# A two-layer graph network on one core: edge groups taken in descending order throughout, node steps in the same iteration, the last four node blocks step by step together

## The chip, the core and the metric

The kernel runs on one core of a Trainium2 chip. Its engines work side by side: TensorE (PE, with PEld for its weight loads) multiplies matrices into PSUM, VectorE (DVE) and ScalarE (ACT) do elementwise work, GpSimd (POOL) issues the indirect DMAs that gather rows, and SyncE (SP) issues plain DMAs, as ACT does too. The metric is the device time of one launch in microseconds; less is better.

## The reference

There are N = 30000 nodes with D = 128 features and E = 960000 edges, sorted by their destination. Layer 0 is a pair of relational graph convolutions with 32 relations built from 8 bases. Layer 1 is a gated convolution with 4 edge types.

```python
dst = minimum((30000 * uniform(960000) ** 2.0).astype(int32), 29999)   # then sorted
# convolution of layer 0, twice, with relu between:
W = einsum('rb,bdf->rdf', coeff, basis)
msg = einsum('nd,rdf->nrf', h, W)[src, etype] * norm
agg = segment_sum(msg, dst, num_segments=N) + bias
# layer 1, for each of T = 4 types:
k, q, v = x @ Wk[t] + bk[t], x @ Wq[t] + bq[t], x @ Wv[t] + bv[t]
msg = where(edge_type == t, sigmoid(k[dst] + q[src]) * v[src], 0)
out_t = segment_sum(msg, dst) + x @ Ws[t] + b[t]
# the result is the mean over t; both layers take relu(layernorm(x)) and add x
```

## The kernel before

**Tiles and groups.** Edges come in tiles of 128, three tiles (G = 3) make a group of GE = 384 edges, and there are NGR = 2500 groups. Edges are sorted by destination, so a group's destinations lie within a window of W = 32 nodes. Sums live in `agg`, one SBUF tile of 128 features by NX columns, a column per node; `add_windows` (L356) adds the 32-column result of a group to the columns that start at the group's first destination. Those starts are read from memory into registers (`bases`, L345), so DVE knows them only at run time.

**Passes.** `edge_pass` (L296) runs three times: c1 (first convolution), c2 (second) and g (gated layer). Each is a hardware loop (L312) of NI = 25 iterations with NG = 100 groups each. In an iteration of c1 and c2 (`rel_body`), each group gathers its three tiles of rows with one indirect DMA a tile (`gather`, L113; 15,000 in the two passes), builds selection matrices on DVE (L439), multiplies on PE (L445), copies on ACT (L449), and for every five groups multiplies with the bases (L407) and adds five windows (L359). In g (`gate_body`), each group gathers rows of `qvtab` (7,500 in all), forms keys (L499), adds, takes the sigmoid (L541), multiplies (L508), sums by destination (L510) and adds windows.

**Node steps.** When the sums of a node are complete, its columns have to be turned into rows and prepared for the next pass. That is done in blocks of VB = 120 nodes, and each pass has its own list of steps with a position for each: `after_first` (L556) adds a bias, takes relu, transposes, stores rows of `h1` and resets the columns to x plus a bias; `after_second` (L587) takes the layer norm and computes the tables `ktab` and `qvtab` with three 512-wide multiplications; `after_third` (L673) transposes and stores the output. An iteration carries NPI / VB = 10 blocks: block u's steps stand beside groups u x PERIOD + n, with PERIOD = 9 and n the step's position (L317 to L325). The order inside an iteration is written out by hand (`manual_schedule`); tile pools give the number of buffers.

**Order.** The host reverses the 25 stretches of edges, so that iteration 0 has the edges with the highest destinations; inside a stretch the groups ascend. An iteration's node blocks cover nodes whose sums were completed by earlier iterations: block u of iteration i starts at column N + LAG + 120 u - 1200 i, with LAG = 240. In iteration 0 those columns lie above N, in padding. After the loop the lowest NPI + LAG = 1440 columns are left: 12 blocks, taken one after another in program order (L328 to L332), with three buffers for most tiles (two for `xt` and `xs`) and six PSUM banks. POOL has no gathers to issue in that time, and the next pass reads the tables that the last blocks write.

**A check ahead.** Before the passes, the kernel tests on the chip that the destinations allow this order (L227 to L249): all of a group's destinations within its window, and no stretch's last group reaching columns that were already worked off. If a test fails, a general path (`any_path`, L732) runs instead of `sorted_path`.

Of the kernel before, what the change touches and what calls it, by code (L numbers as in the profile page):

```python
# [44 lines left out]
VB = 120  # L45
NPI = N // NI
PERIOD = NG * VB // NPI - 1
LAG = 2 * VB
NX = N + NPI + LAG
GAP = 8  # L50
EPS = 1e-5
CH = 5
# [17 lines left out]
def kernel(  # L70
# [114 lines left out]
    with tc.tile_pool(name="prep", bufs=2) as prep, tc.tile_pool(name="pre", bufs=4) as pre, \  # L185
            tc.tile_pool(name="prep_ps", bufs=1, space=PSUM) as prep_ps:
        lo = prep.tile([TP, CH], F32, name="lo", bufs=1)
        hi = prep.tile([TP, CH], F32, name="hi", bufs=1)

        def edge_chunk(c):  # L190
            ts = slice(c * CT, (c + 1) * CT)
            fi = prep.tile([TP, CG], I32, name="fi")
            nc.sync.dma_start(fi, rows_of(first[c * CG:(c + 1) * CG], TP))
            dch = prep.tile([TP, CT], I32, name="dch")
            nc.sync.dma_start(dch, dst[:, ts])
            rch = prep.tile([TP, CT], F32, name="rch")
            nc.vector.tensor_tensor(
                rch.rearrange("p (g j) -> p g j", j=G),
                dch.rearrange("p (g j) -> p g j", j=G),
                fi.unsqueeze(2).to_broadcast([TP, CG, G]),  # L200
                ALU.subtract,
            )
            nc.vector.tensor_reduce(lo[:, c:c + 1], rch, AX.X, ALU.min)
            nc.vector.tensor_reduce(hi[:, c:c + 1], rch, AX.X, ALU.max)
            nc.scalar.dma_start(reld[:, ts], rch)

        def node_chunk(i):
            xt = pre.tile([P, KN, D], F32, name="xt")
            nc.sync.dma_start(xt, step(x, i))
            st = pre.tile([P, KN, 6], F32, name="st")  # L210
            mv = pre.tile([P, KN, 2], F32, name="mv")
            for k in range(KN):
                nc.vector.bn_stats(st[:, k, :], xt[:, k, :])
                nc.vector.bn_aggr(mv[:, k, :], st[:, k, :])
            rs = pre.tile([P, KN], F32, name="rs")
            nc.scalar.activation(rs, mv[:, :, 1], AF.Sqrt, bias=eps)
            nc.vector.reciprocal(rs, rs)
            off = pre.tile([P, KN], F32, name="off")
            nc.vector.scalar_tensor_tensor(off, mv[:, :, 0], -1.0, rs, op0=ALU.mult,
                                           op1=ALU.mult)  # L220
            h = pre.tile([P, KN, D], F32, name="h")
            for k in range(KN):
                nc.scalar.activation(h[:, k, :], xt[:, k, :], AF.Relu, scale=rs[:, k:k + 1],
                                     bias=off[:, k:k + 1])
            nc.scalar.dma_start(step(h0, i), h)

        for c in range(CH):  # L227
            edge_chunk(c)
            for i in range(c * STEPS // CH, (c + 1) * STEPS // CH):
                node_chunk(i)  # L230
        bad = prep.tile([TP, 2, CH], F32, name="bad", bufs=1)
        nc.vector.tensor_scalar(bad[:, 0, :], lo, 0.0, None, op0=ALU.is_lt)
        nc.vector.tensor_scalar(bad[:, 1, :], hi, float(W - 1), None, op0=ALU.is_gt)
        nbad = prep.tile([TP, 1], F32, name="nbad", bufs=1)
        nc.vector.tensor_reduce(nbad, bad, AX.XY, ALU.add)
        at = prep.tile([NI, NG], I32, name="at", bufs=1)
        nc.sync.dma_start(at, first.rearrange("(i g) -> i g", i=NI))
        last = prep.tile([NI, 1], F32, name="last", bufs=1)
        nc.vector.tensor_reduce(last, at, AX.X, ALU.max)
        even = prep.tile([NI, 1], F32, name="even", bufs=1)  # L240
        nc.gpsimd.iota(even, pattern=[[0, 1]], base=N + LAG - W, channel_multiplier=-NPI,
                       allow_small_or_imprecise_dtypes=True)
        late = prep.tile([NI, 1], F32, name="late", bufs=1)
        nc.vector.tensor_tensor(late, last, even, ALU.is_gt)
        nc.vector.tensor_add(nbad[:NI], nbad[:NI], late)
        pbad = prep_ps.tile([1, 1], F32, name="pbad")
        nc.tensor.matmul(pbad, lhsT=nbad, rhs=ones[:TP], start=True, stop=True)
        nc.vector.tensor_copy(flag, pbad)
    n_bad = nc.values_load(flag[0:1, 0:1], min_val=0, max_val=2 * CH * TP + NI)  # L249


    def node_weights(nodew):
# [39 lines left out]


    def sorted_path():
        with ExitStack() as all_:
            def edge_pass(name, body, after, banks, extra=None):  # L296


                with ExitStack() as held:
                    weights = held.enter_context(tc.tile_pool(name=f"{name}_w", bufs=1))  # L300
                    steps, run = after(weights), body(weights)
                    with tc.tile_pool(name=f"{name}_io", bufs=NQ) as io, \
                            tc.tile_pool(name=f"{name}", bufs=2) as pool, \
                            tc.tile_pool(name=f"{name}_n", bufs=1) as npool, \
                            tc.tile_pool(name=f"{name}_nps", bufs=banks, space=PSUM) as nps, \
                            tc.tile_pool(name=f"{name}_c", bufs=1, space=PSUM) as cps, \
                            tc.tile_pool(name=f"{name}_ps", bufs=2, space=PSUM) as ps:
                        cp = cps.tile([P, 4 * D], F32, name="cp")
                        iw, ic = cp[:, :W], cp[:, W:W + 1]
                        nc.vector.tensor_copy(iw, irow)  # L310
                        nc.vector.tensor_copy(ic, icol)
                        with tc.For_i(0, NI, 1, iteration_sync="staggered") as i:  # L312
                            with tc.manual_schedule():
                                todo = {}
                                for n, step_ in extra(i, npool) if extra else ():
                                    todo.setdefault(n, []).append(step_)
                                for u in range(NPI // VB):  # L317
                                    at = i * -NPI + (N + LAG + u * VB)
                                    for n, step in steps(at, npool, nps):
                                        todo.setdefault(u * PERIOD + n, []).append(step)  # L320
                                assert W < TQ * 4 * B and max(todo) < NG

                                def beside(n):
                                    for step in todo.get(n, ()):
                                        step()  # L325

                                run(i, io, pool, ps, cp, iw, ic, beside)
                    with tc.tile_pool(name=f"{name}_l", bufs=3) as lpool, \  # L328
                            tc.tile_pool(name=f"{name}_lps", bufs=6, space=PSUM) as lps:
                        for at in range(0, NPI + LAG, VB):  # L330
                            for _, step in steps(at, lpool, lps):
                                step()  # L332

            def leave_stage():
# [220 lines left out]

            def after_first(weights):  # L556

                def steps(at, pool, ps):
                    xt = pool.tile([VB, D], F32, name="xt", bufs=2)
                    r = pool.tile([P, VB], F32, name="r")  # L560
                    h = pool.tile([VB, D], F32, name="h")
                    cols, rows = agg[:, ds(at, VB)], ds(at, VB)
# [24 lines left out]
            def after_second(weights):  # L587
# [6 lines left out]
                nc.vector.tensor_reduce(bsc, b4, AX.X, ALU.add)  # L594
                nc.vector.tensor_scalar(bsc, bsc, 1.0 / T, None, op0=ALU.mult)

                def steps(at, pool, ps):
                    cols, rows = agg[:, ds(at, VB)], ds(at, VB)
                    xs = pool.tile([P, VB], F32, name="xs", bufs=2)
                    st = pool.tile([VB, 6], F32, name="st")  # L600
                    mv = pool.tile([VB, 2], F32, name="mv")
                    rs = pool.tile([VB, 1], F32, name="rs")
# [69 lines left out]

            def after_third(weights):  # L673

                def steps(at, pool, ps):
                    c = pool.tile([P, VB], F32, name="c")
                    o = pool.tile([VB, D], F32, name="o")
                    got = {}

                    def copy():  # L680
                        nc.scalar.copy(c, agg[:, ds(at, VB)])  # L681

                    def turn():
                        got["pr"] = ps.tile([VB, D], F32, name="pr")
                        nc.tensor.transpose(got["pr"], c, ident)  # L685

                    def back():
                        nc.scalar.copy(o, got["pr"])  # L688

                    def store():  # L690
                        nc.scalar.dma_start(out[ds(at, VB), :], o)  # L691

                    return (1, copy), (3, turn), (4, back), (5, store)
# [268 lines left out]
```

## Time and profile before

| | us |
|---|---|
| median of three timed runs | 28902.54 (28895.52 to 28908.87) |
| the profiled execution's own time | 34449.25 |
| its span | 34447.5 |
| stretch of c1's loop (215 to 11386) | 11171 |
| stretch of c2's loop (11432 to 22748) | 11316 |
| stretch of g's loop (22865 to 34420) | 11555 |
| mean granted PE clock | 0.674 |

The span runs from the first to the last instruction of one recorded execution. That execution is longer than the timed ones; its durations and the order of its events are what the views show. In lines of the views, L445 is line 445 of the kernel, `out<-in` are tile names, "xN" is a count, and square brackets give the idle time of the engine ahead of an instruction with what ended it. "issue" is idle time in which nothing shown was waited for, and "remote" is a releaser that the record does not name.

### The profile page before, as it was taken

What the parts mean: (1) busy time and instruction counts of PE and PEld (TensorE: products, weight loads), DVE (VectorE), ACT (ScalarE), POOL (GpSimd) and SP (SyncE); (2) the same over time, 40 slices, a digit from 0 to 9 for tenths busy, and PEclk for the clock granted to TensorE, in tenths of its full rate; (3) what the DMA queues carried; (4) which work ended last, traced back from release to release, by engine and by line L of the source; (5) the groups of instructions that cost most, each with busy time, mean ns of one, the idle gap of its engine ahead of it and who ended that gap; (6) DMA issues with size and microseconds to landing.
All of it is one profiled execution on the core that took longest, in us unless ns stands there. A gap on an engine that the chain in (4) does not pass through costs nothing. (4 is left out here: it accounts for less than half of the span.)

```text
span 34447.5 us, 320361 instructions
## 1 busy us (share of the span) xinstructions
PE 20497.2 (60%) x87408; PEld 17662.1 (51%) x87408; DVE 12592.8 (37%) x33274; ACT 3659.3 (11%) x9905; POOL 21410.1 (62%) x22514
## 2 busy tenths in 40 slices
PE   4555555555555566666666666665555555555555
PEld 3444544444444445545555454445555555555555
DVE  3333333333333333333333333333333333333333
ACT  1000000000000111111111111111111111111111
POOL 5666666666666566666666666656666666666666
PEclk7777777777777777777777777765555555555555
DMA  3222222222222222222222222234444444444444
GB/s 97 62 62 62 63 61 62 63 63 62 62 62 62 70 73 73 73 74 72 72 73 73 73 73 73 73 107 145 145 144 144 144 144 146 145 144 144 146 143 141
DMA packets 2182999, 3244.35 MB, mean 94 GB/s; under 512 B 551918, under 2 KB 1559594, under 8 KB 2181290
## 3 DMA queue, kind: packets, MB, share of 16 engines
q0 software_dynamic: 840000, 1967.52, 20.6%
q1 hardware_dynamic: 993620, 1001.65, 9.0%
q10 hardware_dynamic: 347670, 254.20, 2.6%
q8 instruction: 852, 13.96, 0.2%
q14 instruction: 857, 7.02, 0.1%
HBM read 2969.29 MB, written 252.28 MB: 94 GB/s over the span
## 5 line engine op out<-in xcount | busy, mean ns | idle before, releaser
L114 POOL DMA_INDIRECT hg<-h,idx x15000 | 14273.0, 952 | 8446.5 <-issue 4105.1
L445 PE MATMUL pa<-sb,hg 128*128 128x256 f32 x30000 | 9304.2, 468 | 5934.2 <-issue 2892.9
L445 PEld LDWEIGHTS pa<-sb,hg 128*128 128x128 f32 x30000 | 6919.2, 240 | 7715.2 <-issue 3346.1
L114 POOL DMA_INDIRECT qv<-qvtab,qi x7500 | 7109.3, 948 | 4562.6 <-issue 2220.3
L439 DVE SCALAR_TENSOR_TENSOR sb<-cp,relc,ce 128x256 f32<-128x256 f32 x15000 | 6134.1, 476 | 6576.0 <-remote 4679.9
L510 PE MATMUL po<-sel,msg 128*128 128x32 f32 x15000 | 3471.0, 388 | 4592.1 <-DVE msg L508 3824.5
L510 PEld LDWEIGHTS po<-sel,msg 128*128 128x128 f32 x15000 | 3420.4, 328 | 4894.5 <-DVE msg L508 3986.6
L499 PE MATMUL pk<-kw,kb 128*128 128x128 f32 x15000 | 3973.5, 438 | 219.5 <-DVE kb L486 178.4
L540 DVE TENSOR_TENSOR pk<-pk,qv 128x384 f32<-128x384 f32 x2500 | 1406.8, 563 | 7074.9 <-remote 4837.9
L449 ACT COPY ab<-pa 128x256 f32<-128x256 f32 x5000 | 1816.6, 373 | 20148.8 <-remote 8809.6
L499 PEld LDWEIGHTS pk<-kw,kb 128*128 128x128 f32 x15000 | 3466.7, 331 | 222.3 <-issue 222.3
L407 PE MATMUL po<-ab,bas 128*128 128x160 f32 x16000 | 2431.3, 306 | 311.2 <-ACT ab L449 262.8
L407 PEld LDWEIGHTS po<-ab,bas 128*128 128x128 f32 x16000 | 2356.8, 196 | 408.4 <-ACT ab L449 291.0
L359 DVE TENSOR_TENSOR agg<-agg,po 128x32 f32 x7500 | 1402.9, 187 | 2742.5 <-remote 709.7
L541 ACT ACTIVATE pk<-pk 128x384 f32<-128x384 f32 x2500 | 1186.7, 475 | 9493.7 <-DVE pk L540 6531.3
L390 PE MATMUL cp<-coeff,oh 128*128 128x32 f32 x8000 | 1313.4, 297 | 1472.0 <-issue 1173.2
L390 PEld LDWEIGHTS cp<-coeff,oh 128*128 128x128 f32 x8000 | 1394.2, 237 | 1530.9 <-issue 1308.1
L637 PE MATMUL bank<-wall,hT 128*120 128x512 f32 x1572 | 1012.0, 765 | 710.2 <-issue 307.3
L508 DVE TENSOR_TENSOR msg<-pk,qv 128x384 f32<-128x384 f32 x2500 | 1368.0, 548 | 19.4 <-remote 19.4
L486 DVE TENSOR_TENSOR kb<-kb,cp 128x1920 f32<-128x1920 f32 x500 | 1072.7, 2145 | 52.0 <-issue 29.6
L637 PEld LDWEIGHTS bank<-wall,hT 128*120 128x120 f32 x1572 | 345.9, 235 | 988.0 <-issue 581.2
L648 DVE TENSOR_TENSOR kt<-bank,ball 120x512 f32<-120x512 f32 x262 | 181.2, 692 | 1484.0 <-remote 509.2
(77 smaller groups left out, 3762.9 us busy)
## 6 DMA issues: line engine op xcount, KB each, us to landing
kb<-kcode SPq DMA_DIRECT2D x500, 960.0 KB
er<-in_et_row SPq DMA_DIRECT2D x1000, 256.0 KB
hg<-h,idx POOLq DMA_INDIRECT x15000
kw<-ktab SPq DMA_DIRECT2D x2500, 64.0 KB
qvtab<-qvt ACTq DMA_DIRECT2D x262, 480.0 KB
qv<-qvtab,qi POOLq DMA_INDIRECT x7500
ktab<-kt ACTq DMA_DIRECT2D x262, 240.0 KB
xt<-in_x SPq DMA_DIRECT2D x262, 60.0 KB
```

Of the source, the lines that this page charges most:

```text
L114: nc.gpsimd.indirect_dma_start(out=to, out_offset=None, in_=table, in_offset=bass.IndirectOffsetOnAxis(ap=idx, axis=0))
L359: nc.vector.tensor_add(to, to, po[:, g, :])
L390: nc.tensor.matmul(pc[s][:, c].rearrange("p q b -> p (q b)"), lhsT=oh[s][:, c, :], rhs=cof.rearrange("p q b -> p (q b)"), start=True, stop ...
L407: nc.tensor.matmul(po[s].rearrange("p s w -> p (s w)"), lhsT=bas[:, b, :], rhs=ab[s][:, b].rearrange("p s w -> p (s w)"), start=(b == 0), ...
L439: nc.vector.scalar_tensor_tensor(sb, iw[:TP].unsqueeze(1).to_broadcast([TP, B, W]), relc[:, t0 + j:t0 + j + 1], ce[s].rearrange("p q c b - ...
L445: nc.tensor.matmul(pa.rearrange("p b w -> p (b w)"), lhsT=hg[:, j, :], rhs=sb.rearrange("p b w -> p (b w)"), start=(j == 0), stop=(j == G ...
L449: nc.scalar.copy(ab[s][:, :, g, :], pa)
L499: nc.tensor.matmul(pk[n][:, j, :], lhsT=kb[n // S][:, n % S, j * TP:(j + 1) * TP], rhs=kw[n], start=True, stop=True)
L508: nc.vector.tensor_mul(msg, pk[n], qv[n][:, :, 1, :])
L510: nc.tensor.matmul(po[s][:, g, :], lhsT=msg[:, j, :], rhs=sel[s][:, g * G + j, :], start=(j == 0), stop=(j == G - 1))
L540: nc.vector.tensor_add(pk[n], pk[n], qv[n][:, :, 0, :])
L637: nc.tensor.matmul(bank(a, VB, T * D), lhsT=hT, rhs=wall[:, a].rearrange("p t f -> p (t f)"), start=True, stop=True)
```

## The change

The host reverses the order of all 2500 groups, not that of 25 stretches, so destinations descend from group to group within an iteration as well. The node blocks follow inside the same iteration: block u of iteration i starts at column N + LAG - 120 (u + 1) - 1200 i, with LAG = 480. An assertion on the host says that the blocks stay behind the additions by at most LEAD = 360 columns. The test on the chip compares every group's first destination with its own limit, where it compared each stretch's highest one. After the loop 480 columns are left, 4 blocks, and they are taken together: the first step of all four, then the second step of all four, and so on, with four buffers for each tile and eight PSUM banks.

```diff
-LAG = 2 * VB
-NX = N + NPI + LAG
+LAG = 4 * VB
+NX = N + LAG
+LEAD = 3 * VB
...
-        last = prep.tile([NI, 1], F32, name="last", bufs=1)
-        nc.vector.tensor_reduce(last, at, AX.X, ALU.max)
-        even = prep.tile([NI, 1], F32, name="even", bufs=1)
-        nc.gpsimd.iota(even, pattern=[[0, 1]], base=N + LAG - W, channel_multiplier=-NPI,
-                       allow_small_or_imprecise_dtypes=True)
+        even = prep.tile([NI, NG], F32, name="even", bufs=1)
+        nc.gpsimd.iota(even, pattern=[[-NPI // NG, NG]], base=N + LAG - LEAD - W,
+                       channel_multiplier=-NPI, allow_small_or_imprecise_dtypes=True)
+        nc.vector.tensor_tensor(even, at, even, ALU.is_gt)
         late = prep.tile([NI, 1], F32, name="late", bufs=1)
-        nc.vector.tensor_tensor(late, last, even, ALU.is_gt)
+        nc.vector.tensor_reduce(late, even, AX.X, ALU.add)
...
+        for u in range(NPI // VB):
+            late = min(g for g in range(NG)
+                       if min((g // S + 2) * S + S - 2, NG) > u * PERIOD + 1)
+            assert (u + 1) * VB - late * NPI // NG <= LEAD
...
                                 for u in range(NPI // VB):
-                                    at = i * -NPI + (N + LAG + u * VB)
-                                    for n, step in steps(at, npool, nps):
+                                    at = i * -NPI + (N + LAG - (u + 1) * VB)
+                                    for n, step in steps(at, npool, nps, 2):
                                         todo.setdefault(u * PERIOD + n, []).append(step)
...
-                    with tc.tile_pool(name=f"{name}_l", bufs=3) as lpool, \
-                            tc.tile_pool(name=f"{name}_lps", bufs=6, space=PSUM) as lps:
-                        for at in range(0, NPI + LAG, VB):
-                            for _, step in steps(at, lpool, lps):
+                    left = LAG // VB
+                    with tc.tile_pool(name=f"{name}_l", bufs=left) as lpool, \
+                            tc.tile_pool(name=f"{name}_lps", bufs=8, space=PSUM) as lps:
+                        for together in zip(*(steps(at, lpool, lps, left)
+                                              for at in range(0, LAG, VB))):
+                            for _, step in together:
                                 step()
...
-                def steps(at, pool, ps):
-                    xt = pool.tile([VB, D], F32, name="xt", bufs=2)
+                def steps(at, pool, ps, deep):
+                    xt = pool.tile([VB, D], F32, name="xt", bufs=deep)
...
-                def steps(at, pool, ps):
+                def steps(at, pool, ps, deep):
...
-                    xs = pool.tile([P, VB], F32, name="xs", bufs=2)
+                    xs = pool.tile([P, VB], F32, name="xs", bufs=deep)
...
-        return np.ascontiguousarray(v.reshape(NI, -1)[::-1]).reshape(-1)
+        return np.ascontiguousarray(v.reshape(NGR, GE)[::-1]).reshape(-1)
```

More of the change, by code (lines that the diff above doesn't have):

```diff
@@ L248 @@
         nc.vector.tensor_copy(flag, pbad)
-    n_bad = nc.values_load(flag[0:1, 0:1], min_val=0, max_val=2 * CH * TP + NI)
+    n_bad = nc.values_load(flag[0:1, 0:1], min_val=0, max_val=2 * CH * TP + NGR)
     def node_weights(nodew):
@@ L673, in after_third, with steps @@
             def after_third(weights):
-                def steps(at, pool, ps):
+                def steps(at, pool, ps, deep):
                     c = pool.tile([P, VB], F32, name="c")
```

## The prediction

> **What bounds the kernel now.** First the head of the page: which engine sets the pace, and is it the same one throughout?
>
> ```profile
> PE 20497.2 (60%) x87408; PEld 17662.1 (51%) x87408; DVE 12592.8 (37%) x33274; ACT 3659.3 (11%) x9905; POOL 21410.1 (62%) x22514
> ...
> POOL 5666666666666566666666666656666666666666
> PEclk7777777777777777777777777765555555555555
> ```
>
> No engine is full, and POOL holds one level through all three passes: it issues 22,500 gathers. The wait table of POOL says what lies between them.
>
> ```profile
> POOL hg L114 <- issue: 4105.1, 12309, 164.1
> POOL qv L114 <- issue: 2220.3, 6716, 4.5
> POOL hg L114 <- remote: 1988.1, 816, 3.8
> POOL qv L114 <- DVE msg L508: 1761.6, 473, 15.1
> ...
> POOL qv L114 <- DMA qi<-qidx: 121.1, 3, 117.2
> ...
> POOL hg L114 <- DMA idx<-in_src: 44.5, 1, 44.5
> ```
>
> The columns are total us, times, longest. Two lines hold one very long wait each: 44.5 and 117.2 us. The timeline of POOL puts them at 11387.4 to 11431.9 and at 22748.0 to 22865.2, between one pass and the next. They are the places where the blocks left over after a loop are worked off, with no gather to run beside them. The view by stretches, cut there (columns: us; busy time and instructions of PE, PEld, DVE, ACT, POOL; PE clock; DMA share; GB/s):
>
> ```profile
> 11395.00:11412.00 17.00, 7.68 (x24) 3.64 (x24) 4.06 (x12) 6.78 (x24) 0.00 (x0) 0.53 0.32 84
> 11412.00:11432.00 20.00, 0.00 (x0) 0.00 (x0) 3.26 (x10) 0.00 (x0) 0.13 (x1) 0.50 0.50 129
> 22748.00:22756.00 8.00, 3.78 (x20) 2.80 (x20) 1.88 (x10) 1.25 (x5) 0.03 (x1) 0.98 0.03 10
> 22756.00:22856.00 100.00, 64.85 (x120) 27.49 (x120) 31.59 (x86) 15.79 (x47) 0.00 (x0) 0.73 0.33 84
> 22856.00:22865.00 9.00, 0.00 (x0) 0.00 (x0) 0.00 (x0) 0.00 (x0) 0.00 (x0) 0.61 0.26 66
> 34430.00:34448.00 18.00, 4.48 (x12) 2.11 (x12) 0.00 (x0) 6.87 (x25) 0.00 (x0) 0.50 0.20 47
> ```
>
> So the left-over blocks cost about 17 us after c1, 100 us after c2 and 18 us after g, all with POOL at zero. In c2 the blocks go one after another; one of the twelve in the timeline:
>
> ```profile
> 22783.76 5.47 PE L637 MATMUL bank<-wall,hT 128*120 128x512 f32 x6 [0.36 <-ACT hT L633]
> ...
> 22789.27 0.69 DVE L648 TENSOR_TENSOR qvt<-bank,ball 120x512 f32<-120x512 f32 x1 [2.72 <-PE bank L637]
> ...
> 22790.12 0.29 DVE L620 BATCH_NORM_STATS2 st<-bank 120x6 f32<-120x128 f32 x1
> ...
> 22791.52 0.41 DVE L626 TENSOR_SCALAR hn<-bank,mv,rs 120x128 f32<-120x128 f32 x1
> ...
> 22792.34 0.27 ACT L633 ACTIVATE hT<-bank 128x120 f32<-128x120 f32 x1 [0.88 <-PE bank L630]
> ...
> 22792.67 0.75 PE L637 MATMUL bank<-wall,hT 128*120 128x512 f32 x1 [0.36 <-ACT hT L633]
> ```
>
> The next block's statistics (22790.12) start only after this block's weights, and its own weights at 22792.67, 8.9 us after this one's. PE waits through norm, turn and relu every time.
>
> [...] six weight matmuls of a left-over block take 5.47 us in some blocks and 2.84 us in others, a ratio of 1.93. [...] Here 84 GB/s filled a share of 0.33, thus an estimated 255 GB/s when full. [...] loops are fetched anew: the instruction queues q8 and q14 moved 20.98 MB[...]. [...] ACT_TABLE_LOAD: [...] the trace has 1283, once ahead of g's left-over blocks, and it stays.
>
> **Part by part.** The sum is against the profiled execution (34449.25 us, span 34447.5). The runs' median is 28902.54, 5546.7 us less, or 0.247 us for each of the 22,500 gathers. I take this as recording cost of the gathers; the left-over blocks have none, so their savings count in full in both.
>
> *Loops.* Per iteration there are ten blocks before and after, at the same places (u x PERIOD + n, PERIOD still 9), with the same instructions; only the constant in the row address differs, and bufs=2 is what they had. The DMAs of a moved block (xt on SP, stores on ACT) are the same, on the same queues, past the same instructions. Two things might change. First, blocks now read columns that this iteration's adds have just written. But the trace of before already makes them wait: "ACT c L681 <- DVE agg L359" 40 times, 38.6 us together, though those columns lay outside this iteration's windows. Ordering goes by the tile, so no new wait: 0. Cover if wrong: a block's copy stands at n = 1 + 9u, adds at n = 3, 8, 13... (4, 9, 14... in g), mostly a group or more earlier; a group is 3 gathers, 3.75 us. Second, the order of groups: same counts, sizes, and still random sources: 0. Placement of the later loops' code: bound below.
>
> *Preparation.* The agg memset shrinks by 960 of 31440 columns (26.3 us x 3% = 0.8), on POOL, idle until 192 us. The test on "at" has three instructions either way (0.235 + 0.147 + 0.122 us before); a 25x100 compare is of the size of the 0.235. Sum: 0.
>
> *After c1.* Before: 11395.06 (first xt load) to 11411.65 (end of the last store), 16.6 us, paced by xt loads with two buffers. After: four loads at once. The first landed after 3.6 us, the second 0.47 later; four at this step land by 5.1. Then transpose 0.46, DVE 0.34, last store issue 0.34, with hand-overs 0.2: about 6.5. Saves 10 (8 to 11).
>
> *After c2.* Before: 22755.67 to 22856.02, 100.35 us. After, by phases of four blocks, in us from the first copy:
> - copies and transposes; DVE's first statistics at 2.7 as before (an unexplained idle that I keep);
> - statistics 4 x (0.33 + 0.21) = 2.2, to 4.9; norm 4 x (0.20 + 0.41) = 2.4, to 7.3; last turn and relu to 7.8;
> - 24 weight matmuls. The twelve blocks took 2.84 to 5.47 for six, mean 4.58. [...] I take 3.75 a block: 15.0. The bounds are 4 x 2.84 = 11.4 and 4 x 5.47 = 21.9. Four "part" at 0.4: 1.6. PE ends at 24.4;
> - biases and copies (4 x 2 x 0.69 on DVE, 4 x 0.59 on ACT) lie beside PE; store issues, 8 x 0.90 = 7.2 on ACT, half beside it, and the last qvtab issue ends at about 27.5.
>
> Eight banks carry it: the first reuse is w0 on px's bank, released at norm. Drain: four blocks are 2.88 MB; the last 1.92 MB at 255 GB/s take 7.5 us, of which 3 stick out. 100.35 - 27.5 - 3 = 70 (62 to 78). Late next is the loop start: last store to first gather took 9 us and stays.
>
> *After g.* Before: 34430.4 to 34443.94, and 3.5 us of landing. Table load 1.28, then blocks of 1.1 us. After: 1.28 + four copies 0.9 + transpose and copy 0.7 + four copies and stores 2.3 = 5.2, then landing. 13.5 - 5.2 = 8 (6 to 9).
>
> Sum 10 + 70 + 8 = 88 us: profiled 34449 - 88 = 34361; timed 28902.5 - 88 = **28,815**, 0.30% less. With the ends, 76 to 98 us; adding 20 us of loop scatter either way, 28,785 to 28,845.
>
> **Rivals.**
> - *Stores bound c2's end.* If 2.88 MB go at the 84 GB/s seen, 34 us from the first store issue (about 16): end at 50, c2 saves 50, sum 68: 28,835. For: 512-byte to 1-KB pieces on one queue. Against: g's loop moves 145 GB/s.
> - *Code placement shifts loop stalls.* c2's and g's loops move by the removed blocks' instructions. PE waited 2892.9 us for "issue" at L445 alone; 3% of it is 87 us either way: 28,902 or 28,728. For: code is refetched every iteration. Against: most of these idle times lie beside waits of DVE and ACT, not alone.
> - *Slower: the add-to-read wait becomes real.* Place: the first ACT instruction of each of the 750 loop blocks, behind the five DVE adds of a group; queued behind it are ACT's ab copies (or sigmoids), for which PE and then the gather buffers wait. Price: five adds, 1.07 us, if POOL pays all: 750 x 1.07 = 802, minus 88: 29,617. It decides from 88 / 750 = 0.12 us a block. Against: these waits exist already.
> - *The change doesn't do what it says*: the new test fails and the general path runs, many times slower. With dst about 30000 q squared, group k of the reversed order starts near 30000 (1 - (k+1)/2500) squared, the limit is 30088 - 12k: the margin is 112 at k = 0, 100 at the end and larger between. I put it under 1%, inside the slower case.
>
> **How the numbers follow.** Forecast 0.65; stores 0.09 (0.07 still faster by over 0.2%, 0.02 within); placement 0.16 (0.06 faster, 0.07 within, 0.03 slower); slower 0.10. About 0.2%, 58 us, is what a measurement of this kernel can tell from no change. Faster 0.78, same 0.09, slower 0.13. The range reaches from the placement gain to the placement loss, 28,725 to 28,900, and leaves out the slower case.
>
> **What would show it.** POOL's two long waits should read about 34 us (from 44.5) and 47 us (from 117.2); the stretch from g's last add to the end about 10 us (from 18); L637 should count 1524 instead of 1572; the three loops should last 11171, 11316 and 11555 us within 20 each. A c2 gap over 60 us with ACT stores or DMA last says the stores rival; loops longer by the same amount in every iteration with more waits between L359 and L614, L569 or L681 say the slower one; shifts in c2 and g but not c1 say placement.

## The result and the profile after

| us | before | after |
|---|---|---|
| median of six timed runs each | 28901.8 (28882.95 to 28912.14) | 28781.38 (28775.14 to 28806.21) |
| ratio, 95% interval | | 0.996 (0.9949 to 0.9971) |

The changed kernel is faster by 120 us; the interval of the ratio, times 28902, says 84 to 147. The forecast was 28,815, so 88 us, at the small end of that.

One thing must be known before the traces are compared. The profiled execution of the changed kernel has a span of 28780.1 us, and its 28781.85 is one of the six timed runs; that of the kernel before had 34447.5. The experiments below ran on three chips on which the kernel before needs 34.2 ms in its timed runs as well (medians 34193.18, 34193.29 and 34212.23); on which chip the first results were taken is not recorded. So there are two paces, 28.8 and 34.2 ms. The loops of two traces are set against each other only where both have one pace, and times only among runs that share a chip: e0 to e3, e4 to e7, and f1 to f4.

The waits of POOL in the kernel after (columns: total us, times, longest; lines have moved down by one to seven, so the gather is L115):

```profile
POOL hg L115 <- issue: 3861.4, 12112, 165.9
...
POOL qv L115 <- DVE msg L515: 246.3, 234, 4.9
...
POOL qv L115 <- DMA qi<-qidx: 38.5, 1, 38.5
POOL hg L115 <- DMA idx<-in_src: 34.5, 1, 34.5
```

The two long waits, 44.5 and 117.2 us in the kernel before, are 34.5 and 38.5 here. The stretches of the same kernel around the left-over blocks of c2 and g (columns as in the table by stretches above):

```profile
19102.00:19126.00 24.00, 16.33 (x40) 7.59 (x40) 9.81 (x30) 5.11 (x16) 0.00 (x0) 0.79 0.34 92
...
19123.00:19126.00 3.00, 0.00 (x0) 0.00 (x0) 1.03 (x5) 0.00 (x0) 0.00 (x0) 1.00 0.98 317
...
28765.00:28781.00 16.00, 1.21 (x5) 0.70 (x4) 0.93 (x5) 3.04 (x9) 0.00 (x0) 0.50 0.10 24
```

The 100 us of c2 have become 24, with PE busy for 16.33 of them. That is some 68%, against 65% before: most of what was saved is work that no longer stands there. The timeline of the kernel after shows how the four blocks follow each other there:

```profile
19102.71 0.87 ACT L621 COPY xs<-agg 128x120 f32<-128x120 f32 x4 [4.64 <-PEq L317]
...
19107.63 1.61 PE L637 MATMUL bank<-ident,hn 120*128 120x120 f32 x4 [1.14 <-DVE hn L633]
...
19109.10 12.84 PE L644 MATMUL bank<-wall,hT 128*120 128x512 f32 x24
19110.07 0.32 PEld L644 LDWEIGHTS bank<-wall,hT 128*120 128x120 f32 x1 [0.53 <-ACT hT L640]
...
19114.06 0.18 PEld L644 LDWEIGHTS bank<-wall,hT 128*120 128x120 f32 x1 [0.25 <-issue]
...
19120.17 4.91 ACTq L660 DMA_DIRECT2D qvtab<-qvt  x4
...
19133.67 0.94 POOL L115 DMA_INDIRECT qv<-qvtab,qi  x1 [38.49 <-DMA qi<-qidx]
```

Each step stands there once for four blocks (x4, x24): one train of 24 weight matmuls with no gap in it, where before there were twelve trains with PE waiting ahead of each. From the first copy to the end of the last store issue (19120.17 + 4.91) it takes 22.4 us. The transfers run on until about 19128 at almost full DMA use (a share of 0.98 from 19123 to 19126 and of 1.00 from 19126 to 19128), and the next pass's first gather follows 8.6 us after the last issue; in the kernel before it was 9.2.

### The profile page after: what moved, and what is told of

Same layout as the page of the kernel before. It is cut to its first block, busy times and chain, and to the rows that moved or that the text cites. A ratio compares the mean times of both kernels' runs of the same rounds, so it can differ in the third digit from the quotient of the medians.

```text
span 28780.1 us, 320078 instructions
## 1 busy us (share of the span) xinstructions
PE 21221.5 (74%) x87304; PEld 17145.2 (60%) x87304; DVE 12629.5 (44%) x33210; ACT 3700.4 (13%) x9841; POOL 21324.5 (74%) x22514
## 4 chain that ended last, share of the span: by engine, by line
## 5 line engine op out<-in xcount | busy, mean ns | idle before, releaser
L115 POOL DMA_INDIRECT hg<-h,idx x15000 | 14208.4, 947 | 4859.0 <-issue 3861.4
L452 PE MATMUL pa<-sb,hg 128*128 128x256 f32 x30000 | 9846.7, 461 | 4313.7 <-DMA hg<-h,idx 2922.9
L452 PEld LDWEIGHTS pa<-sb,hg 128*128 128x128 f32 x30000 | 6085.6, 225 | 7351.0 <-issue 3776.2
L115 POOL DMA_INDIRECT qv<-qvtab,qi x7500 | 7089.2, 945 | 2573.4 <-issue 2018.2
L414 PEld LDWEIGHTS po<-ab,bas 128*128 128x128 f32 x16000 | 2781.5, 225 | 140.6 <-ACT ab L456 53.6
L414 PE MATMUL po<-ab,bas 128*128 128x160 f32 x16000 | 2815.6, 338 | 23.1 <-ACT ab L456 23.1
L397 PEld LDWEIGHTS cp<-coeff,oh 128*128 128x128 f32 x8000 | 1335.0, 238 | 455.0 <-issue 327.7
L397 PE MATMUL cp<-coeff,oh 128*128 128x32 f32 x8000 | 1247.3, 307 | 356.9 <-DVE oh L392 356.9
L644 PE MATMUL bank<-wall,hT 128*120 128x512 f32 x1524 | 861.7, 681 | 4.5 <-issue 4.5
L392 DVE TENSOR_SCALAR oh<-er,icol 128x512 f32<-128x512 int32 x1000 | 492.6, 493 | 83.9 <-issue 59.7
```

Of the source, the lines that this page charges most:

```text
L115: nc.gpsimd.indirect_dma_start(out=to, out_offset=None, in_=table, in_offset=bass.IndirectOffsetOnAxis(ap=idx, axis=0))
L397: nc.tensor.matmul(pc[s][:, c].rearrange("p q b -> p (q b)"), lhsT=oh[s][:, c, :], rhs=cof.rearrange("p q b -> p (q b)"), start=True, stop ...
L414: nc.tensor.matmul(po[s].rearrange("p s w -> p (s w)"), lhsT=bas[:, b, :], rhs=ab[s][:, b].rearrange("p s w -> p (s w)"), start=(b == 0), ...
L452: nc.tensor.matmul(pa.rearrange("p b w -> p (b w)"), lhsT=hg[:, j, :], rhs=sb.rearrange("p b w -> p (b w)"), start=(j == 0), stop=(j == G ...
```

## The experiments

In each, the loops, waits and tail come from the times of the gathers in the trace: a loop runs from the first gather of a pass to the end of its last, gap 1 and gap 2 are POOL's pauses between the loops, the tail lies after the last gather. All times are in us. The medians are over 10 to 21 executions, and over 43 to 53 of the kernel before on each chip; the parts in the last two columns are read from one recorded execution of each run.

| run | median | before, same chip | difference | ratio (95%) | gap 1 / gap 2 / tail | loops c1, c2, g |
|---|---|---|---|---|---|---|
| e0_before | 34189.64 | 34193.18 | -3.5 | 1.0000 (0.9992-1.0008) | 43.7 / 124.0 / 27.6 | 11076.7, 11157.2, 11566.9 |
| e1_groups | 34178.73 | 34193.18 | -14.4 | 0.9996 (0.9988-1.0004) | 45.0 / 122.7 / 28.0 | 11082.9, 11175.1, 11557.4 |
| e2_single | 34125.67 | 34193.18 | -67.5 | 0.9979 (0.9970-0.9987) | 34.0 / 50.2 / 23.2 | 11087.9, 11190.0, 11546.2 |
| e3_fours | 34148.51 | 34193.18 | -44.7 | 0.9989 (0.9982-0.9995) | 43.0 / 82.1 / 28.1 | 11056.1, 11176.3, 11544.3 |
| e4_before | 34207.26 | 34193.29 | +14.0 | 1.0004 (0.9996-1.0013) | 45.2 / 125.8 / 27.4 | 11049.8, 11181.4, 11545.9 |
| e5_after | 34110.76 | 34193.29 | -82.5 | 0.9981 (0.9972-0.9990) | 33.0 / 40.8 / 21.6 | 11062.2, 11204.2, 11537.4 |
| e6_groups | 34196.39 | 34193.29 | +3.1 | 1.0001 (0.9994-1.0007) | 46.3 / 121.1 / 27.5 | 11045.9, 11175.4, 11527.1 |
| e7_weights | 34225.95 | 34193.29 | +32.7 | 1.0009 (1.0002-1.0016) | 18.2 / 40.1 / 21.4 | 11063.8, 11330.4, 11535.3 |
| f1_before | 34218.29 | 34212.23 | +6.1 | 1.0000 (0.9992-1.0009) | 48.0 / 122.0 / 28.3 | 11068.3, 11191.9, 11551.4 |
| f2_after | 34117.54 | 34212.23 | -94.7 | 0.9973 (0.9963-0.9982) | 30.5 / 42.5 / 23.2 | 11056.8, 11187.1, 11552.7 |
| f3_weights | 34247.95 | 34212.23 | +35.7 | 1.0006 (0.9998-1.0015) | 16.8 / 42.1 / 19.9 | 11051.5, 11360.2, 11553.5 |
| f4_shift | 34156.87 | 34212.23 | -55.4 | 0.9984 (0.9976-0.9991) | 42.9 / 38.6 / 23.5 | 11087.6, 11174.8, 11628.7 |

My theory: all of the gain lies between and after the loops, most of it after c2, and the loops are untouched. The rivals: the descending groups alone change the loops; or code placement does; or the number of blocks left makes all of it and taking them together adds nothing.

**The kernel before again (e0, e4, f1).** No edit: these show the scatter of the loops and give the traces that the others stand against.

> The kernel before, unaltered, recorded again: the profiled execution on record is 5.5 ms longer than its timed runs, so its loops cannot be set against those of the changed kernel. Forecast's theory (all of the gain is at the ends of the passes): about 28902 us, ratio 1.000; POOL's two long waits are about 44 and 117 us as in the first record, and from the first to the last gather the loops take what they take in the changed kernel, 9426 (c1), 9441 (c2) and 9624 us (g), within 10 each. Rival (the loops became faster too, by the new order or by where their code lies): one or more of the loops is longer by some 10 to 30 us, 20 to 35 in sum.

> The kernel before again, for a record on the same chip as the changed kernel beside it. In the first round on a chip the kernel before took 34190 us with loops of 11077, 11157 and 11567 us; the changed kernel's record has 9426, 9441 and 9624. Theory: ratio 1.000, POOL's long waits 44 and 117 to 124 us, and the three loops as long as the changed kernel's in the same call within 20 us in sum. Rival: they are longer by 20 us or more in sum.

> The kernel before, once more beside the changed kernel. So far the two waits and the tail are 198 us in it and 95 us in the changed kernel, and the loops of the two are equal within the scatter of about 30 us. Theory: again 195 to 202 us, and loops equal to the changed kernel's in this call within 30 us in sum. Rival: loops longer by more than 30 us.

The time and the loops that were expected for e0 did not come: it took 34.19 ms, not 28902 us, and its loops are 1650 to 1943 us longer than those of the first trace of the kernel after. The sum of the three loops was 33800.8, 33777.1 and 33811.6: one kernel scatters by 35 us. The first record of the kernel before, at 34447.5 us, lies further off still: counted in the same way, its loops are 11194.8, 11316.2 and 11554.7, 34065.7 together. The two gaps and the tail together were 195.3, 198.4 and 198.3, a scatter of 3 (189.3 in the first record). A saving between the loops can be read to a few us, one of 20 us inside the loops cannot.

**The kernel after on these chips (e5, f2).** The whole change.

> The changed kernel on the same chip as the kernel before. Theory: POOL's long waits 34.5 and 38.5 us and a tail of 22 us after the last gather, as in its first record, so 94 to 100 us less than the kernel before in this call; loops equal. Rival: about 120 us less, with the other 20 us in the loops, and then more in c2 and g (code moved) than in c1, or in all three (order of the groups).

> The changed kernel. Theory: two waits and tail 93 to 98 us, about 103 us less than the kernel before in this call; where a launch takes 28.9 ms that is a ratio of 0.9964, where it takes 34.2 ms 0.9970. Rival (something in the loops gains too): 120 us or more.

The waits of POOL, the kernel before (f1) first:

```profile
POOL qv L114 <- DMA qi<-qidx: 122.0, 1, 122.0
...
POOL hg L114 <- DMA idx<-in_src: 48.0, 1, 48.0
```

and the kernel after (f2), with two lines that are needed below:

```profile
POOL qv L115 <- DVE msg L515: 1769.1, 442, 16.1
POOL hg L115 <- PE pa L452: 1002.1, 628, 13.6
...
POOL qv L115 <- DMA qi<-qidx: 42.5, 1, 42.5
...
POOL hg L115 <- DMA idx<-in_src: 30.5, 1, 30.5
```

Gaps and tail come to 95.4 (e5) and 96.2 (f2), and to 95.3 in the first trace of the kernel after, on the quicker chip. Against 198.4 and 198.3 that is 103 and 102 us less: about 80 to 85 of it after c2, 12 to 17 after c1, 5 to 6 after g. The loops came out at 33803.8 and 33796.7, within the scatter of before. The timed differences, 82.5 and 94.7, are under 102, and the 120 of the first result is over it. The intervals of the first result (84 to 147) and of f2 (62 to 127) hold 102; that of e5, 34 to 96, ends just below it.

**Only the order of the groups (e1, e6).** The kernel before, with all groups reversed by the host and nothing else; one kernel on two chips.

```diff
-        return np.ascontiguousarray(v.reshape(NI, -1)[::-1]).reshape(-1)
+        return np.ascontiguousarray(v.reshape(NGR, GE)[::-1]).reshape(-1)
```

> One part alone: the kernel before with all 2500 groups reversed by the host; node steps, left-over blocks and every instruction as before. Theory: the order of the groups costs nothing, 28902 us, ratio 1.000. Rival (the order makes the loops faster): 20 to 35 us less, about 28875, ratio 0.999.

> Group order alone, again, on the chip of the two kernels beside it. Theory: ratio 1.000, loops as in the kernel before within 20 us in sum. Rival (order of the groups makes loops faster): 20 us less or more, spread over all three loops.

The times differ by -14.4 and +3.1 us, both intervals hold 1, and gaps and tail are as before. The loops in sum are 15 us longer than in e0 and 29 us shorter than in e4; by e6's trace alone the rival would have come true, but the opposite signs say scatter. So no effect of the order by itself shows at this pace: what it does is to permit the late node blocks. The rival's 20 to 35 us less are unlikely, though the interval of e1 (41 us less to 14 more) doesn't shut them out.

**Four blocks, one after another (e2).** The kernel after, with the last four blocks as the kernel before takes them: three buffers (two for `xt` and `xs`) and six banks.

```diff
-                    with tc.tile_pool(name=f"{name}_l", bufs=left) as lpool, \
-                            tc.tile_pool(name=f"{name}_lps", bufs=8, space=PSUM) as lps:
-                        for together in zip(*(steps(at, lpool, lps, left)
-                                              for at in range(0, LAG, VB))):
-                            for _, step in together:
+                    with tc.tile_pool(name=f"{name}_l", bufs=3) as lpool, \
+                            tc.tile_pool(name=f"{name}_lps", bufs=6, space=PSUM) as lps:
+                        for at in range(0, LAG, VB):
+                            for _, step in steps(at, lpool, lps, 2):
```

> The changed kernel with its four left-over blocks taken one after another, with the buffers and banks of before. Theory: the number of blocks is the larger part. In c2 four blocks at 8.3 us and a start of 3 us take about 36 us against 22 together, in c1 and g 1 to 2 us more than together: about 28781 + 17 = 28798 us, ratio to before 0.9964. Rival (taking them together is the larger part of the gain): 28830 us or more.

Gap 2 is 50.2, against 124.0 in e0 and 40.8 and 42.5 with the four together (e5, f2). So going from twelve blocks to four is worth 74 us of some 83 there, and taking four together another 8 to 9; this smaller part is read from single traces, where gap 2 of one kernel scatters by 4 to 5 us. After c1 and g the single blocks do as well as the four together (34.0 and 23.2 against 33.0 and 21.6, 30.5 and 23.2). Gaps and tail are 107.4, 88 us under e0; the timed 67.5 has an interval of about 44 to 103. The timeline of e2's four trains of weight matmuls:

```profile
22518.02 5.47 PE L642 MATMUL bank<-wall,hT 128*120 128x512 f32 x6 [0.36 <-ACT hT L638]
...
22526.95 4.53 PE L642 MATMUL bank<-wall,hT 128*120 128x512 f32 x6 [0.36 <-ACT hT L638]
...
22535.04 4.13 PE L642 MATMUL bank<-wall,hT 128*120 128x512 f32 x6 [0.36 <-ACT hT L638]
...
22542.60 2.83 PE L642 MATMUL bank<-wall,hT 128*120 128x512 f32 x6 [0.36 <-ACT hT L638]
```

From start to start it is 8.9, 8.1 and 7.6 us. The trains take 16.96 us together, and between them PE transposes for the next block and waits 2.1 to 2.4 us for its norm and 0.36 for its relu. With the four together (the first trace of the kernel after) the 24 matmuls take 12.84 us with nothing between.

**Twelve blocks, in three sets of four together (e3).** The kernel before, with the other half of the change.

```diff
...
-                    with tc.tile_pool(name=f"{name}_l", bufs=3) as lpool, \
-                            tc.tile_pool(name=f"{name}_lps", bufs=6, space=PSUM) as lps:
-                        for at in range(0, NPI + LAG, VB):
-                            for _, step in steps(at, lpool, lps):
-                                step()
+                    with tc.tile_pool(name=f"{name}_l", bufs=4) as lpool, \
+                            tc.tile_pool(name=f"{name}_lps", bufs=8, space=PSUM) as lps:
+                        for four in range(0, NPI + LAG, 4 * VB):
+                            for together in zip(*(steps(at, lpool, lps, 4)
+                                                  for at in range(four, four + 4 * VB, VB))):
+                                for _, step in together:
+                                    step()
...
```

> The kernel before with its order and its twelve left-over blocks, but these taken in three sets of four, step by step together, with four buffers and eight banks. Theory: the steps of four overlap, so a set takes some 17 to 20 us in c2, 57 us instead of 100; c1 and g gain some 3 us each: about 28902 - 48 = 28854 us, ratio 0.9983. Rival (each set has to wait for the buffers of the last, no overlap between sets): three times 22 to 28 us in c2, 28870 us or more.

The wait of POOL after c2 in e3:

```profile
POOL qv L114 <- DMA qi<-qidx: 82.1, 1, 82.1
```

That is 42 us less than in e0, and the timed runs say 44.7 (17 to 61): the expected size. The expected small gains after c1 and g did not come (43.0 and 28.1 against 43.7 and 27.6). Together e2 and e3 show two parts that overlap: 74 and 42 us alone, 83 in one, as what is saved on each block can only be saved on blocks that are left. Both runs change the order of the steps, the buffers and the banks at once, so which of the three is needed was not told apart.

**Weights of c2 loaded ahead of c1 (e7, f3).** In the kernel after, gap 1 still holds the loads of c2's weights, from 9637.67 to the first index load at 9651.64 (14.0 us). I moved them ahead of c1. The theory said that gap 1 falls by them; the rival, that they are hidden or cost as much elsewhere.

```diff
+            early = all_.enter_context(tc.tile_pool(name="early", bufs=1))
+            second = after_second(early)
+            run_second = rel_body(h1, basis[1], coeff[1])(early)
...
-            edge_pass("c2", rel_body(h1, basis[1], coeff[1]), after_second, 2)
+            edge_pass("c2", lambda weights: run_second, lambda weights: second, 2)
```

> The changed kernel, with c2's weights and bases loaded before c1 instead of between the passes. Theory: what is left of the first long wait is mostly these loads; from the first weight load to the first index load it is 14.0 us in the changed kernel's record, so the wait falls from 34.5 to about 21 us and the time by 14 us, ratio to before 0.9955 where the changed kernel has 0.996. Rival (the loop cannot start before the stores of h1 have landed anyway): no more than 5 us less.

> c2's weights before c1, again. In its first run the first long wait fell from 33 to 18 us as expected, but c2's loop grew by 126 us, 5.3 us at the start of each of the 25 iterations. In that loop the DVE and ACT instructions are the same, with 170 and 122 more semaphore waits. Theory: the growth comes from these waits and is there again, 100 us or more in c2's loop, so slower than the changed kernel. Rival (it belonged to that chip or to chance): c2's loop as in the changed kernel, and 15 us less than it.

Gap 1 fell by 14.8 and 13.7 us, and yet the kernel lost 115 and 130 us against e5 and f2. Some 8 us are a later first gather (202.2 against 193.9 in f2). The rest is c2's loop: +126 and +173 us. The waits of POOL in f3 show where, against the lines of f2 above:

```profile
POOL hg L115 <- PE pa L452: 1175.2, 626, 14.3
...
POOL hg L115 <- DMA idx<-in_src: 16.8, 1, 16.8
```

As many waits for `pa` as before (626 against 628), and 173 us more in them. By place in the iteration (mean us of five groups, from the gathers' times over 25 iterations of c2):

```
groups     e5_after   e7_weights   f2_after   f3_weights
0 to 4      28.70       33.80        28.69      34.44
5 to 9      19.12       19.11        19.15      19.18
10 to 14    23.18       23.09        23.26      23.08
15 to 19    22.81       23.11        23.01      23.21
```

The first five groups after the loop's branch, where engines start an iteration again, hold 5.10 x 25 = 127 us in e7, where the loop grew by 126, and 5.75 x 25 = 144 of the 173 in f3. In that loop DVE also has 170 and ACT 121 more semaphore instructions than in the kernel after. The packets of the instruction queues q8 and q14 in c2's loop are the same (274 and 158 in e7, 274 and 157 in e5), so no more code is fetched there. Whether the added waits, the changed place of the code or that of the weights in SBUF holds PE up was not told apart. The gain of 14 us in the gap was real, and what it set off cost some ten times as much, at this pace. At the quick pace the move was not run; there the first trace of the kernel after has 18.89 us for groups 0 to 4 of c2 and 18.77 to 18.80 for the next three fives, so a start of the iteration as dear as here isn't in it.

**Code shifted, nothing else (f4).** Forty tiny instructions on each of PE, DVE, ACT and POOL between c1 and c2. They are executed once; the loops of c2 and g only come to stand elsewhere. This is the placement rival by itself.

```diff
...
+                for _ in range(40):
+                    nc.vector.memset(sv, 1.0)
+                    nc.scalar.copy(sa, ones)
+                    nc.gpsimd.memset(sg, 1.0)
+                    nc.tensor.matmul(sp, lhsT=ones, rhs=ones, start=True, stop=True)
```

> The changed kernel with 40 tiny instructions on each of PE, DVE, ACT and POOL between c1 and c2 (results unused), so that the code of c2's and g's loops lies elsewhere while their instructions and waits stay. Theory (the place of the code costs nothing): 3 to 10 us more than the changed kernel, all in the first long wait; loops within 30 us in sum. Rival (placement shifts loop stalls): c2's or g's loop moves by 30 us or more, either way.

Gap 1 grew by 12 us, which are the forty. The loop of c2 became 12 us shorter (11174.8), and g's became 11628.7, 76 us over f2, with the same number of instructions and of semaphore waits on every engine. By place it is again the first five groups: 36.03 us against 33.01, 3.0 x 25 = 75, every later five within 0.4 of f2. The waits of POOL in f4, against f2's:

```profile
POOL qv L115 <- DVE msg L515: 1961.5, 481, 17.6
...
POOL hg L115 <- DMA idx<-in_src: 27.7, 1, 27.7
```

POOL waits 192 us longer for `msg` than in f2. Other waits of POOL shrink against it, as the one for `pk` from 379.4 to 261.8. c1's loop, which stands ahead of the edit, is 31 us longer too; that is the scatter.

How much of the 76 belongs to the edit is open. The recorded execution of f4 is the second slowest of its 18 and that of f2 the second fastest of its 10, 104 us apart, while the medians are 39 us apart. Of these 39 the gap takes 12, which leaves some 27 for the loops. The place within the iteration speaks for the edit: groups 0 to 4 of g take 32.6 to 33.8 us in the eleven other traces of e0 to f3. But in the first record of the kernel before they take 29.6 with no edit at all. What the trace does show is that the fetching of code changed: the instruction queues q8 and q14 carried 249 and 303 packets in g's loop, against 273 and 399 in f2. So less was fetched while the loop came out longer, and more fetching is not the cause.

No kernel of these runs was quicker than the changed kernel.

## Why the prediction came out right, and where its terms were off

The direction, the place and the mechanism were right; the time was within the range. Its size was in part luck. The terms summed to 88 us, 76 to 98 with their ends, where traces of one pace show 102 to 103 and the timed runs 120. The measured 28,781 lies just below the 28,785 to 28,845 that the terms and the scatter of the loops gave; it is in the range because this was drawn down to 28,725 for a gain by placement, which no run shows to have come.

- *After c1, 10 us forecast.* From the first `xt` load to the end of the last store issue it took 6.4 us (forecast 6.5), gap 1 fell from 44.5 to 34.5. Right. In the later pairs it fell by 12.2 and 17.5, above the 8 to 11 that were given; why is not known.
- *After c2, 70 us forecast.* The order of what ends last was right: weight matmuls, then store issues. The terms were too careful by 9 to 15 us (gap 2 fell by 78.7 between the first two traces, by 79.5 and 85.0 in the later pairs). To the last issue it took 22.4 us instead of 27.5. The first weight matmul came 6.4 us after the first copy (forecast 7.8), and the 24 took 12.84 us (forecast 15.0, inside its bounds of 11.4 and 21.9). The largest mis-sized term of these is that price of 3.75 a block; 3.21 is measured. It was my estimate, between the 2.84 us of the quickest of the twelve blocks and their mean of 4.58. In the trace of the kernel after, a weight load takes 0.32 us early in the train, which starts at 19109.10, and 0.18 from 19114.06 on, and the granted clock is 0.50 from 19109.1 to 19113.7 and 1.00 from 19113.8 to 19122. So the clock was at 0.50 for the first 4.6 us of the train, and did not go back to it within the train. The 3 us of stores sticking out weren't there in the sense of the sum: the transfers do run on for some 3 us, but the kernel before has such a drain, 2.9 us, inside its 9.2 us from last issue to first gather, and in the changed kernel that stretch, at 8.6, is no longer. The sum had counted it twice.
- *After g, 8 us forecast.* 5 to 6 came, and from g's last addition to the end it took 13.9 us where about 10 were forecast (18.3 before). The term that I missed is an idle 3.75 us on ACT between the second and third output, in this timeline of the kernel after:

```profile
28768.69 0.87 ACT L688 COPY c<-agg 128x120 f32<-128x120 f32 x4
...
28769.83 0.35 ACTq L698 DMA_DIRECT2D out_x<-o  x1
28773.76 0.27 ACT L695 COPY o<-pr 120x128 f32<-120x128 f32 x1 [3.75 <-DMA out_x<-o]
...
28774.33 1.94 ACTq L698 DMA_DIRECT2D out_x<-o  x2
```

  PE had finished the four transposes at 28770.14, and every `o` has a buffer of its own, so no data explains it. The idle comes again in e5 (3.47 us) and f2 (3.84). In the first trace five packets of the instruction queues, 48 KB, move between 28770.6 and 28771.9, inside the idle; the kernel before has an idle of 2.4 us on ACT (34438.31 to 34440.73) in the same stretch, also with such packets (34438.9 to 34440.4), which the sum took for work. A wait for code would fit, but the packets don't name the engine that they were for, so the cause isn't shown.
- *Loops, 0 forecast.* Right as far as it can be seen. Instruction counts in c1's loop are the same on every engine, in c2's they differ by at most 10, in g's by 177 semaphore instructions (100 of them on ACT) among some 110,000. Traces of e0 to f2 give 33777 to 33812 before and 33797 to 33804 after. But the test that the prediction set, 11171, 11316 and 11555 within 20 each, failed for c1 and c2 at either pace, and the kernel before fails it too (e0: 11076.7, 11157.2, 11566.9): it was taken from one record. The add-to-read wait (the slower rival, 0.12 us a block to decide) cost nothing that shows in these sums.
- *Stores as the bound after c2.* Wrong rival: the price of 84 GB/s was that of a stretch in which DMA had little to do. When four blocks' stores were there at once, the stretch 19123 to 19126 moved 317 GB/s at a share of 0.98, in pieces of 512 and 1024 bytes as in the kernel before. The estimate of 255 GB/s when full, scaled up from those 84 GB/s at a share of 0.33, was low too.
- *Placement.* Perhaps a real mechanism (f4; e7 has more waits beside), of up to 76 us in one recorded execution and some 27 in the medians, where I gave 87 as its bound. That the loops' code is fetched anew is measured: in the first trace of the kernel before, every iteration of c2's loop but the first has 12 packets of the instruction queue q8 and 6 of q14. That fetching stalls the loops was my estimate, and no run shows it. No shift of the loops by placement showed in the change itself: in the traces of e0 to f2, c2's and g's loops before and after differ by 50 us at most, mostly by less than 30.
- *Recording cost, 0.247 us a gather.* Wrong. The gathers take nearly the same in both traces (945 to 947 ns in the quick one, 948 to 952 in the slower, 305 ns between), and 7500 of them at 1.25 us make a floor of 9375 us for a loop; the quick trace is within 3% of it (9426.1, 9440.8, 9624.1). The recorded execution of the changed kernel took 28781.85 us, the median of its timed runs being 28781.38, so recording 22,500 gathers does not cost 5.5 ms; and the kernel before needs 34.2 ms in its later timed runs too. The forecast survived this only because the saved time lies where no gather runs, and gaps and tail are alike at both paces (95.3, 95.4, 96.2).

What stays open: the timed gain was 120 us in the first result, and what the traces show between and after the loops makes 102. The other 18 lie inside the interval (84 to 147), but a small gain in the loops at the quick pace can't be excluded, since there is no trace of the kernel before at that pace.

## What to carry to other kernels

When an engine that paces a loop pauses between two loops, the work in the pause costs its full length, so first let less be left over (74 us here), and then take what is left step by step together, which paid here only where a chain of dependent steps let the busiest engine idle (8 to 9 us after c2, nothing after c1). An interval outside the loops can be summed from durations (88 us here, where 102 were read), and a change of that size in a loop of tens of thousands of instructions can't: leave its scatter to the range, and look at it by place in the iteration before blaming the edit. Moving loads out of a gap is no free gain; look at the loops that follow.

## What the runs showed of the hardware

- One program ran at two paces, 28.8 and 34.2 ms. In the trace of the kernel after at 28.8 ms, 95% of SP's 5251 FUSED_REGOPS (instructions that only work on registers) take up to 60 ns, and in that of the same kernel at 34.1 ms (f2) up to 706, at medians of 46 and 51; their sum is 268 against 1051 us. Gathers are nearly alike. The granted PE clock is not the reason: in g's loop it is 0.51 in both, and the loop takes 9624.1 and 11552.7 us. Three chips had the slower pace; whether it belongs to the chip, and what makes it slow, isn't shown.
- At the slower pace the start of an iteration is dear and touchy: groups 0 to 4 took 28.7 us in c2 and 33.0 in g, where 15 gathers at 1.25 take 18.8 (f2), and edits outside the loop went with 3.0 (f4) and 5.10 and 5.75 us more (e7, f3). At the quick pace the same groups took 18.9 and 22.2 us. Each of q8's packets is of 16,384 bytes (828 in the first trace of the kernel after). With an edit outside g's loop other numbers of packets were fetched in it (249 of q8 and 303 of q14 in f4, 273 and 399 in f2); that fetching sets the time isn't shown.
